# A rebuilt prologue in a fused cross-attention and ternary feed-forward kernel: rotary table spread by TensorE, first stacks written inside SBUF

## The chip, the cores and the metric

The kernel runs on one core of one Trainium2 chip. The metric is the device time of one execution in microseconds (us). The engines are TensorE (PE: matrix products and transposes), VectorE (DVE), ScalarE (ACT), GpSimd (POOL) and SyncE (SP), which here only issues transfers; ACT issues a few as well.

## The reference

`x` is 4 x 512 x 512, the context 4 x 512 x 256, all float32, with two positions in [0, 1) per token. The core of it:

```
x = x + xattn(layernorm(x), ctx, pos, pos, Wq, Wkv, Wout, bout)
x = x + ffn(layernorm(x), w_fc, w_proj)

xattn: q = rope(xn @ Wq), k, v = split(ctx @ Wkv), k = rope(k)     # 32 heads of 16
       softmax(q k^T / 4) v @ Wout + bout
rope:  ang = pos * freqs (2 positions x 4 frequencies per head)
       (x1, x2) -> (x1 cos - x2 sin, x1 sin + x2 cos)
ffn:   bitlinear(gelu(bitlinear(x, w_fc)), w_proj)   # layer norm, ternary weights
```

## The kernel before

**Stages.** Attention runs first, as one stream over 32 groups (4 batches x 8 groups of 4 heads), then the feed-forward part with all weights in SBUF. For attention the rotated queries and keys are each split in a high part (float32r) and a low part (the rest), and both are stacked on the partitions, 64 rows per head, so that one float32r product over 64 rows gives full accuracy. A group's two tiles `q_st` and `k_st` are its *stacks*. `heads` makes 8 heads' queries or keys: a product on PE, a copy to `rot` on ACT, a swap of row pairs with a stream shuffle into `oth` on DVE, two products with the tables in `trig` and a sum, then `high` and `low`. `store` writes them to the DRAM tensors `q_d` and `k_d`, four row sets of 128 rows each, and `load_stacks` reads two groups' worth back in the stacked order.

**A group.** `logits` (L423) makes one unit of scores (128 queries x 512 keys for two heads), `maxima` (L437) takes their row maxima on DVE. After eight units `place_maxima` transposes the maxima, ACT copies them to `mrows`, and `exponentials` computes the scores transposed (L462), subtracts the maxima by a product with the selector `sel` (L470), and takes Exp on ACT (L474). `weigh` (L484) multiplies by the values. PSUM has three double banks `ps_s`, one `ps_v` for the weighted values and one `ps_t` for all other products.

**Order.** The order on each engine is the order of the program text (a manual schedule over all five engines). `put_off(k, f)` delays an instruction to turn `k`, `run(k)` emits it. In the stream a burst holds three units, and a queue of *chores* (products of later heads, values, projections) is worked off between them by a credit per burst. Logits run up to 12 units ahead of exponentials. In the prologue a chore is finished at once, and `prologue[0]` chooses banks and engines.

**The prologue before.** SP and ACT load x, positions and first weights. `trig_tables` computes the sines of all four batches in one 128 x 256 tile (six DVE instructions, two on ACT), writes them to `trig_d` in DRAM; `load_trig(0)` reads batch 0's tables back, broadcast to all heads. DVE then takes the layer norm statistics (`norm1`), normalises (`normed`), PE transposes (`tokens`). The first two `heads` calls for keys and queries are rotated on DVE, stored to DRAM, and stacks 0 and 1 are loaded from there. The fill is a loop of 11 turns: ten logits units, beside them the four `values` products of batch 0, in the last turn the first `place_maxima`. Then output weights are loaded and the stream begins. Stacks 2 and 3 are loaded in the first group of the stream.

Of the kernel before, what the change touches and what calls it, by code (L numbers as in the profile page):

```python
# [15 lines left out]
P = 128  # L16
HD = 16
# [14 lines left out]
def xattn_ffn(  # L32
# [27 lines left out]
    VS = HD + 1  # L60
    FB = F // 512
    XH = 3
    RATE, RATE_END = 1.3, 1.1
# [26 lines left out]
    rden_d = [dram.tile([NH, S], F32, name=f"rden_d{b}") for b in range(B)]  # L90
    trig_d = dram.tile([2, 2, HD // 2, B * S], F32, name="trig_d")

# [31 lines left out]

    TW = B * S // HD * 2
    trig_sb = apool.tile([P, 4, TW], F32, name="trig_sb", tag="es", bufs=NES)
    pos_sb = trig_sb[:, 0, :]
    load_x(0, 0, 1)  # L130
    for n in range(2):
        nc.scalar.dma_start(
            pos_sb[n * P // 2 : (n + 1) * P // 2, :],
            pos.rearrange("a (c w) -> a c w", w=TW)
            .unsqueeze(0)
            .to_broadcast([4, 2, B * S // TW, TW]),
        )
    for t in range(1, NT):
        load_x(0, t, 1)
    ctx_tiles[0] = apool.tile([P, KC, S], F32, name="c_sb0", tag="c_sb", bufs=1)  # L140
    nc.scalar.dma_start(ctx_tiles[0], ctxT[0].rearrange("(k p) s -> p k s", p=P))
    load_columns(wkv_sb, wkv, 0, P)
    load_columns(wq_sb, wq, 0, P)


    ident = const.tile([P, P], F32, name="ident")
    make_identity(nc, ident)
    ones = const.tile([P, P], F32, name="ones")
    nc.gpsimd.memset(ones, 1.0)
    mhalf = const.tile([P, NT], F32, name="mhalf")  # L150
# [9 lines left out]
    nc.vector.tensor_tensor(row, row, ident, ALU.mult)  # L160
    nc.vector.tensor_reduce(col[:, 0:1], row, AX.X, ALU.add)


# [29 lines left out]
    def rstd(var, scale, eps, n, name):  # L193

        r = small.tile([P, n], F32, name=name, tag=f"rstd{n}")
        nc.gpsimd.tensor_scalar(r, var, scale, eps, ALU.mult, ALU.add)  # L196
        nc.gpsimd.tensor_tensor(r, r, mhalf[:, :n], ALU.pow)
        return r
# [3 lines left out]

    def trig_tables():

        ang, turns, sines = (trig_sb[:, n, :] for n in range(1, 4))
        e = nc.vector
        e.tensor_scalar(ang, pos_sb, col[:, 0:1], col[:, 1:2], ALU.mult, ALU.add)
        e.tensor_scalar(turns, ang, 0.5 / math.pi, ROUND, ALU.mult, ALU.add)
        e.tensor_scalar(turns, turns, ROUND, None, ALU.subtract)
        for part in (TWO_PI_HI, TWO_PI_LO):  # L210
            e.scalar_tensor_tensor(ang, turns, -part, ang, ALU.mult, ALU.add)
        e.tensor_scalar(ang, ang, SIN_MAX, -SIN_MAX, ALU.min, ALU.max)
        half = P // 2
        nc.scalar.activation(sines, ang, AF.Sin)
        nc.scalar.activation(turns[half:, :], ang[half:, :], AF.Sin, scale=-1.0)
        for n, j, src in ((0, 0, sines), (0, 1, sines), (1, 0, turns), (1, 1, sines)):
            nc.sync.dma_start(
                trig_d[n, j].rearrange("r (c w) -> (r c) w", w=TW),
                src[n * half : (n + 1) * half, :],
            )  # L220

    def load_trig(b):
        for n in range(2):
            nc.sync.dma_start(
                trig[:, b % 2, n, :],
                trig_d[n]
                .rearrange("j r t -> (j r) t")[:, b * S : (b + 1) * S]
                .unsqueeze(0)
                .to_broadcast([P // HD, HD, S]),
            )  # L230
# [14 lines left out]

    def bank(name):
        if prologue[0]:
            return ps_s.tile([P, 2, S], F32, name=name, tag="s")[:, 0, :]
        return ps_t.tile([P, S], F32, name=name, tag="t")
# [18 lines left out]
    def normed(b, t):  # L268
        tt = b * NT + t
        mv, r = norms[b]  # L270
        xh[b, t] = apool.tile([P, D], F32, name=f"xh{tt}", tag="xh", bufs=XH)
        nc.vector.tensor_scalar(
            xh[b, t], x_sb[:, tt, :], mv[:, t, 0:1], r[:, t : t + 1], ALU.subtract, ALU.mult
        )
# [18 lines left out]
    class Chore:  # L293


        def __init__(self, name, steps, step, post, cost=1.0, ready=0):
            self.name, self.steps, self.step, self.post = name, steps, step, post
            self.cost, self.ready, self.done = cost, ready, 0

        def go(self):  # L300
            if self.done == 0:
                self.p = bank(self.name)
            self.step(self.p, self.done)
            self.done += 1
            return self.done == self.steps
# [27 lines left out]
    def heads(b, n, what):  # L333
# [9 lines left out]
        def post(p, k):  # L343
            e = nc.vector if prologue[0] else nc.gpsimd
            rot = apool.tile([P, S], F32, name=f"rot_{name}", tag="rot")
            oth = apool.tile([P, S], F32, name=f"oth_{name}", tag="oth")
            high = apool.tile([P, S], F32R, name=f"sh_{name}", tag="sh")
            low = apool.tile([P, S], F32, name=f"sl_{name}", tag="sl")
            dst = (q_d if what == "q" else k_d)[b][n * 4 * P : (n + 1) * 4 * P, :]
            rows = dst.rearrange("(p k) s -> k p s", k=4)  # L350

            def swap():
                nc.vector.stream_shuffle(oth, rot, SWAP)
                e.tensor_tensor(oth, oth, trig[:, b % 2, 1, :], ALU.mult)
                e.tensor_tensor(rot, rot, trig[:, b % 2, 0, :], ALU.mult)
                e.tensor_tensor(rot, rot, oth, ALU.add)
                if not prologue[0]:
                    e.tensor_copy(high, rot)
                    e.tensor_tensor(low, rot, high.bitcast(F32), ALU.subtract)

            def split():
                nc.scalar.copy(high, rot)
                e.tensor_tensor(low, rot, high.bitcast(F32), ALU.subtract)
# [7 lines left out]
            high_f = high.bitcast(F32)  # L371
            hs, ls = ((0, 2), (1, 3)) if what == "q" else ((0, 1), (2, 3))
            put_off(k + 1, lambda: nc.scalar.copy(rot, p))
            put_off(k + 1, swap, 1)
            if prologue[0]:
                put_off(k + 1, split, 1)
            d = 1 if prologue[0] else 4
            put_off(k + d, lambda: store(high_f, hs), 1)
            put_off(k + d + (not prologue[0]), lambda: store(low, ls), 1)

        return Chore(f"{what}p{name}", steps, step, post)

    def values(b, t):
# [289 lines left out]

    k0 = -1000

    def chore(c):
        nonlocal k0
        while not c.go():
            pass
        c.post(c.p, k0)  # L680
        k0 += 1
        run(k0)
        run(k0, 1)

    trig_tables()
    for t in range(NT):
        norm1(0, t)
    load_trig(0)
    load_columns(wkv_sb, wkv, D, 2 * D)
    load_columns(wkv_sb, wkv, P, D)  # L690
    load_columns(wq_sb, wq, P, D)
    for t in range(XH):
        normed(0, t)
    prologue[0] = False
    first_keys = heads(0, 0, "k")
    while not first_keys.go():
        pass
    prologue[0] = True
    for t in range(NT):
        chore(tokens(0, t))  # L700
        if t + XH < NT:
            normed(0, t + XH)
    first_keys.post(first_keys.p, k0)
    chore(heads(0, 0, "q"))
    load_stacks(0)
    load_stacks(1)
    for what in "kq":
        chore(heads(0, 1, what))
    make_sel()
    load_x(1)  # L710
    nc.sync.dma_start(bout_sb, bout.to_broadcast([P, D]))
    prologue[0] = False
    lps = {}
    fill = [values(0, t) for t in range(NT)]
    for n in range(FIRST + 1):
# [6 lines left out]
        run(k0, 1)  # L722
        if fill:
            if fill[0].go():
                fill[0].post(fill[0].p, k0)
                fill.pop(0)
# [4 lines left out]
    assert not fill  # L731
    nc.sync.dma_start(wout_sb, wout.rearrange("(k p) n -> p k n", p=P))
    k0 += 1
# [29 lines left out]
    def projections(b):  # L763
        return [projected(b, t, when((b + 1) * NG + 2, 4)) for t in range(NT)]

    queue = [heads(0, n, w) for n in (2, 3) for w in "kq"]
    queue += sum(prepared(1, when(2)), [])
# [9 lines left out]
    loads_behind = {  # L777
        f"kpk{b}_3": lambda b=b: (load_ctx(b + 1), load_trig(b + 1)) for b in range(B - 1)
    }
    wanted = []  # L780
# [6 lines left out]
    for k, burst in enumerate(bursts):  # L787
        run(k)
        for kind, s in burst:
# [8 lines left out]

            if i == 0 and u in (2, 5):
                wanted.append(2 + u // 4)  # L800
            if u == 6 and 4 <= i + 3 < n_groups:
                wanted.append(i + 3)
            while wanted and {(wanted[0] // NG, wanted[0] % NG // 2, w) for w in "kq"} <= stored:
                load_stacks(wanted.pop(0))
            if i in (0, 4) and u == 0:
                load_x(2 + i // 4)
            if u % 2 == 0 and (b == 0 and g == 0 or b < 2 and g == 5):
# [347 lines left out]
```

## Time and profile before

| | us |
|---|---|
| median of 3 runs (lowest, highest) | 858.34 (857.26, 858.89) |
| profiled execution | 856.57 |
| its span, first to last instruction | 854.8 |
| PE busy in the span | 812.2 |
| DVE, ACT, POOL busy | 619.7, 456.7, 287.1 |
| first logits product starts | 34.37 |
| first exponentials' product starts | 50.66 |
| last exponentials' product starts | 574.9 |

The span is that of one profiled execution; its time is 1.8 us longer than its span and 1.8 us under the median of the runs. PE's busy time includes products at a reduced clock, since the table counts time and not work. Times in the text are from the span's start.

### The profile page before, as it was taken

How to read it: one execution, taken by the hardware profiler on the slowest of the kernel's cores; microseconds unless marked ns; L12 is line 12 of the kernel's file. 1: busy time of each engine (PE TensorE's matmuls, PEld its weight loads, DVE VectorE, ACT ScalarE, POOL GpSimd, SP SyncE). 2: the span in 40 equal slices, each digit the busy share in tenths (PEclk: the TensorE clock that was granted, in tenths of full speed). 3: DMA queues.
4: the chain of work that ended last, by engine and by line, in shares of the span. 5: the costliest groups of instructions: out<-in, count | busy, mean ns of one | idle time of the engine just before them, and what ended most of it. 6: DMA issues, size and time to landing. Idle time of an engine off the chain costs nothing.

```text
span 854.8 us, 13868 instructions
## 1 busy us (share of the span) xinstructions
PE 812.2 (95%) x5364; PEld 428.3 (50%) x5364; DVE 619.7 (72%) x852; ACT 456.7 (53%) x603; POOL 287.1 (34%) x287
## 2 busy tenths in 40 slices
PE   4699999999999899999999999998999999999996
PEld 1134433344333333433333334336668888888885
DVE  4789778788878988878678877825455864864755
ACT  2146766665665545666555665576234544554442
POOL 3017274653833564586515731301000100100000
PEclk9799999999999999999999999999999999999999
DMA  6875777567586576967645657432000100100101
GB/s 205 303 286 194 259 259 228 186 217 262 191 301 200 167 252 220 308 211 264 208 149 183 221 205 272 158 119 98 1 1 1 49 1 1 50 0 1 50 1 49
DMA packets 75561, 135.25 MB, mean 158 GB/s; under 512 B 10728, under 2 KB 12648, under 8 KB 74984
## 3 DMA queue, kind: packets, MB, share of 16 engines
q1 hardware_dynamic: 75088, 133.72, 45.8%
q8 instruction: 42, 0.69, 0.3%
q10 hardware_dynamic: 408, 0.66, 0.2%
q14 instruction: 23, 0.19, 0.1%
HBM read 79.30 MB, written 55.05 MB: 157 GB/s over the span
## 4 chain that ended last, share of the span: by engine, by line
PE 78%; DVE 12%; DMA 6%; issue 1%; ACT 1%; SPq 1%; POOL 1%; ACTq 0%; DVEq 0%; POOLq 0%
PE hp L928 14%; PE fp L966 14%; PE av L484 12%; PE sp L462 7%; PE lp L423 7%; DVE mx L437 7%; PE sp L470 5%; PE qpq L285 4%; PE op L285 4%; PE vp L285 3%; PE kpk L285 3%; PE op L1047 2%; PE mtp L449 1%; DVE ws L583 1%; DMA c_sb<-in_ctxT 1%
## 5 line engine op out<-in xcount | busy, mean ns | idle before, releaser
L437 DVE TENSOR_REDUCE mx<-lp 128x2 f32<-128x1024 f32 x256 | 305.3, 1216 | 86.0 <-PE lp L423 85.6
L474 ACT ACTIVATE es<-sp 128x1024 f32<-128x1024 f32 x256 | 254.5, 1025 | 146.6 <-PE sp L470 138.3
L484 PE MATMUL av<-es,va 128*32 128x512 f32 x1024 | 136.0, 604 | 0.0
L462 PE MATMUL sp<-q_st,k_st 64*128 64x512 f32 x512 | 115.1, 446 | 8.9 <-DVE mx L437 7.7
L423 PE MATMUL lp<-k_st,q_st 64*128 64x512 f32 x512 | 113.0, 437 | 9.4 <-DMA q_st<-q_d 7.4
L936 ACT ACTIVATE h<-hp,gam_fc 128x512 f32<-128x512 f32 x64 | 44.0, 688 | 129.1 <-PE hp L928 129.1
L966 PE MATMUL fp<-wproj,hh 128*128 128x512 f32 x256 | 103.5, 404 | 0.0
L928 PE MATMUL hp<-dTh,wfc 128*128 128x512 f32 x256 | 100.4, 392 | 1.2 <-ACT dTh L657 1.2
L470 PE MATMUL sp<-mrows,sel 64*128 64x512 f32 x512 | 101.2, 390 | 0.2 <-ACT mrows L453 0.2
L966 PE MATMUL fp<-wproj,hl 128*128 128x512 f32 x256 | 101.1, 395 | 0.0
L928 PE MATMUL hp<-dTl,wfc 128*128 128x512 f32 x256 | 100.4, 392 | 0.2 <-DVE dTl L658 0.2
L955 DVE TENSOR_TENSOR acc<-acc,h 128x512 f32<-128x512 f32 x56 | 38.7, 691 | 73.5 <-ACT h L936 73.5
L462 PEld LDWEIGHTS sp<-q_st,k_st 64*128 64x128 f32 x512 | 48.0, 184 | 83.1 <-DVE mx L437 42.6
L423 PEld LDWEIGHTS lp<-k_st,q_st 64*128 64x128 f32 x512 | 48.3, 185 | 80.8 <-ACT es L474 40.3
L523 POOL TENSOR_TENSOR aT<-aT,rb 128x512 f32<-128x512 f32 x16 | 21.1, 1320 | 133.3 <-DMA rb<-rden_d 112.1
L285 PE MATMUL qpq<-xT,wq_sb 128*32 128x512 f32 x512 | 62.3, 594 | 0.8 <-ACT xT L321 0.7
L928 PEld LDWEIGHTS hp<-dTh,wfc 128*128 128x128 f32 x256 | 48.2, 188 | 12.6 <-ACT dTh L657 2.1
L966 PEld LDWEIGHTS fp<-wproj,hl 128*128 128x128 f32 x256 | 48.3, 189 | 11.3 <-issue 0.7
L966 PEld LDWEIGHTS fp<-wproj,hh 128*128 128x128 f32 x256 | 48.2, 188 | 11.2 <-issue 0.7
L928 PEld LDWEIGHTS hp<-dTl,wfc 128*128 128x128 f32 x256 | 48.1, 188 | 11.0 <-DVE dTl L658 0.5
L470 PEld LDWEIGHTS sp<-mrows,sel 64*128 64x128 f32 x512 | 48.5, 185 | 5.9 <-ACT mrows L453 0.9
L196 POOL TENSOR_SCALAR r_a<-mv 128x1 f32<-128x1 f32 x16 | 4.7, 292 | 130.3 <-DVE mv L633 130.3
(129 smaller groups left out, 1036.0 us busy)
## 6 DMA issues: line engine op xcount, KB each, us to landing
k_st<-k_d SPq DMA_DIRECT2D x32, 512.0 KB
q_st<-q_d SPq DMA_DIRECT2D x32, 512.0 KB
k_d<-sh_k SPq DMA_DIRECT2D x32, 256.0 KB
k_d<-sl_k SPq DMA_DIRECT2D x32, 256.0 KB
q_d<-sh_q SPq DMA_DIRECT2D x32, 256.0 KB
q_d<-sl_q SPq DMA_DIRECT2D x32, 256.0 KB
av_d<-avs SPq DMA_DIRECT2D x32, 256.0 KB
wm<-in_wfcT SPq DMA_DIRECT2D x16, 256.0 KB
```

The source lines that it names most:

```text
L285: nc.tensor.matmul(p[j * HP : (j + 1) * HP, :], w[:, j * HP : (j + 1) * HP], x, start=start, stop=stop,)
L423: nc.tensor.matmul(lp[:, h, :], q_st[i][rows, r, t * P : (t + 1) * P], k_st[i][rows, r, :], start=True, stop=True,)
L437: nc.vector.tensor_reduce(mx[i][:, t, :, r], lp, AX.X, ALU.max, negate=True)
L462: nc.tensor.matmul(sp[:, h, :], k_st[i][rows, r, c * P : (c + 1) * P], q_st[i][rows, r, :], start=True, stop=False,)
L470: nc.tensor.matmul(sp[:, h, :], sel[rows, r, :], mrows[i][rows, :], start=False, stop=True)
L474: nc.scalar.activation(es, sp, AF.Exp, scale=1.0 / math.sqrt(HD))
L484: nc.tensor.matmul(av[j * HP : (j + 1) * HP, :], va[b % 2][:, c, v0 : v0 + HP], es[r][:, h, :], start=c == 0, stop=c == NT - 1,)
L523: nc.gpsimd.tensor_tensor(aT[b][:, n, :], aT[b][:, n, :], rb, ALU.mult)
L928: nc.tensor.matmul(hp, wfc_sb[k][:, f * P : (f + 1) * P], dT[b][half][:, k, :], start=half == 0 and k == 0, stop=half == 1 and k == KD - 1,)
L936: nc.scalar.activation(hid[b, f], hp, AF.Gelu, scale=gam_fc[:, 0:1])
L955: nc.vector.tensor_tensor(acc[b][0], old, x, ALU.add)
L966: nc.tensor.matmul(outs[b][t], parts[b, f][half][:, t * P : (t + 1) * P], wproj_sb[f], start=half == 0 and f == 0, stop=half == 1 and f == ...
```

## The change

- **Positions and tables.** The positions of each batch come in a load of their own (four on the ACT queue). `first_trig` computes batch 0's sines only (64 columns), on 128 partitions as 16 rows x 8 chunks. DVE spreads them to a 128 x 512 tile that is zero outside each row's own chunk (`wide`), and PE multiplies that with a 0/1/-1 selector `pick` so that each partition gets its table row; ACT copies the result to `trig`. The tables of batches 1 to 3 are computed later and written to DRAM behind the second stack's load.
- **Warm-up.** 24 products of `ones` by `ones` run on PE ahead of it.
- **Loads.** All of x for batch 0, then context and weights, then x of batch 1 are issued by SP at the start. Bias, output weights and x of batches 2 and 3 are loaded in groups 2, 3, 4 and 8.
- **Statistics.** The variance's epsilon is added on DVE in the prologue, the power stays on POOL. All four normalised tiles are made in a row.
- **First heads and stacks.** `first_heads` rotates the first keys and queries on DVE (keys' cast on ACT, keys' low part on POOL). `first_stacks` writes stack 0 from SBUF to SBUF in 16 transfers of 32 partitions: high parts on the SP queue, low parts on the ACT queue. `second_stacks` writes the other half to DRAM and loads stack 1 from there.
- **Second heads** go through the ordinary `heads`, whose rotation now always runs on POOL. Stacks 2 and 3 are loaded ahead of the stream.
- **Fill.** The first values product runs ahead of the fill; the fill holds the other three, every second one in the `ps_v` bank, and the third keys' product, which leaves the stream's queue. A one-column Exp is emitted before the fill.

```diff
+    for b in range(B):
+        load_pos(nc.scalar, b)
+    for t in range(NT):
         load_x(0, t, 1)
-    nc.scalar.dma_start(ctx_tiles[0], ctxT[0].rearrange("(k p) s -> p k s", p=P))
+    load_ctx(0)
     load_columns(wkv_sb, wkv, 0, P)
     load_columns(wq_sb, wq, 0, P)
+    load_columns(wkv_sb, wkv, P, D)
+    load_columns(wq_sb, wq, P, D)
+    load_columns(wkv_sb, wkv, D, 2 * D)
+    load_x(1)
...
+    def first_trig():
+        at, ang, turns, sines = (trig_sb[:, n, 0, :] for n in range(4))
+        angles(ang, at, turns)
+        nc.scalar.activation(sines, ang, AF.Sin)
+        wide = apool.tile([P, S], F32, name="wide", tag="sl")
+        nc.vector.tensor_tensor(
+            wide.rearrange("p (c w) -> p c w", c=NC),
+            sines.unsqueeze(1).to_broadcast([P, NC, W0]),
+            by_chunk.unsqueeze(2).to_broadcast([P, NC, W0]),
+            ALU.mult,
+        )
+        tp = ps_s.tile([P, 2, S], F32, name="trig_p", tag="s")
+        for n in range(2):
+            product(tp[:, n, :], pick[:, n, :], wide, True, True)
+        for n in range(2):
+            nc.scalar.copy(trig[:, 0, n, :], tp[:, n, :])
...
+    def first_heads(what, p):
+        keys = what == "k"
...
+        nc.scalar.copy(rot, p)
+        e.tensor_tensor(low, p, trig[:, 0, 0, :], ALU.mult)
+        e.stream_shuffle(oth, rot, SWAP)
+        e.tensor_tensor(oth, oth, trig[:, 0, 1, :], ALU.mult)
+        e.tensor_tensor(rot, low, oth, ALU.add)
+        if keys:
+            nc.scalar.copy(high, rot)
+        else:
+            e.tensor_copy(high, rot)
+        (nc.gpsimd if keys else e).tensor_tensor(low, rot, high.bitcast(F32), ALU.subtract)
+        return high.bitcast(F32), low
+
+    def first_stacks(what, high, low):
...
+        for r in range(2):
+            for queue, part, ks in ((nc.sync, high, 0), (nc.scalar, low, 1)):
+                for k in PARTS[what][ks]:
+                    queue.dma_start(
+                        st.bitcast(F32)[k:P:4, r, :], part[r * HP : (r + 1) * HP, :]
+                    )
+
+    def second_stacks():
+        for what in "kq":
...
+            for part, ks in zip(parts[what], PARTS[what]):
+                for k in ks:
+                    nc.sync.dma_start(rows[k], part[2 * HP : 4 * HP, :])
+        load_stacks(1)
...
+    p = bank("warm")
+    for n in range(WARM):
+        product(p[:, 0:P], ones, ones, True, True)
+    first_trig()
+    for t in range(NT):
+        norm1(0, t)
+    for t in range(NT):
+        normed(0, t)
+    store_tables = trig_tables()
+    make_sel()
+    for t in range(NT):
+        c = tokens(0, t)
...
+    for n in range(2):
+        for what in "kq":
+            c = heads(0, n, what)
+            while not c.go():
+                pass
+            if n == 0:
+                parts[what] = first_heads(what, c.p)
+                if what == "q":
+                    first_stacks("k", *parts["k"])
+                continue
...
+            if what == "k":
+                first_stacks("q", *parts["q"])
+            run(k0, 1)
+    second_stacks()
+    store_tables()
...
+    fill = [values(0, t) for t in range(1, NT)] + [heads(0, 2, "k")]
+    for c in fill[::2]:
+        c.spare = True
...
-    nc.sync.dma_start(wout_sb, wout.rearrange("(k p) n -> p k n", p=P))
+    for i in (2, 3):
+        load_stacks(i)
```

## The prediction, made before the changed kernel ran

> **What bounds the kernel now.** The page first: TensorE (PE) is busy 95% of the span, and in its row of 40 slices only the first two are thin. The stretch table of the trace says how thin (columns: stretch, its length, busy time of PE, weight loads, DVE, ACT, POOL, then granted clock, DMA share, GB/s):
>
> ```profile
> 0.00:34.30 34.30, 14.79 (x112) 4.92 (x112) 20.84 (x44) 8.68 (x15) 7.24 (x20) 0.94 0.71 232
> 34.30:50.70 16.40, 15.57 (x90) 3.92 (x90) 11.80 (x15) 2.35 (x4) 0.00 (x0) 0.81 1.04 365
> 50.70:60.00 9.30, 8.30 (x59) 2.81 (x58) 9.23 (x13) 6.43 (x7) 0.00 (x0) 1.00 0.88 323
> 60.00:100.00 40.00, 40.00 (x312) 17.46 (x309) 35.25 (x46) 25.88 (x32) 24.39 (x22) 1.00 0.62 205
> ```
>
> From 60 us on PE has no gap: what comes before it is added to the end one for one. Before 34.3 us PE idles 19.5 us, and from 34.3 to 50.7 it is "busy" at a granted clock of 0.81. The chain of waits says for what (start, length, what):
>
> ```profile
> 1.93 4.24 DMA trig_sb<-in_pos
> ...
> 11.09 2.09 DMA trig_d<-trig_sb
> 13.20 0.03 issue
> 13.23 5.77 DMA trig<-trig_d
> ...
> 27.23 3.49 DMA q_d<-sl_q
> 30.74 0.03 issue
> 30.77 3.46 DMA q_st<-q_d
> 34.23 0.14 issue
> 34.37 0.80 PE lp L423 x2
> ```
>
> The five transfers take 4.24+2.09+5.77+3.49+3.46 = 19.0 us of the first 34.4: positions in, tables out to DRAM and back, rotated heads out and back. The timeline shows the slow clock in identical value products:
>
> ```profile
> 37.68 1.93 PE L285 MATMUL vp<-wkv_sb,c_sb 128*32 128x512 f32 x8
> 40.38 1.06 PE L285 MATMUL vp<-wkv_sb,c_sb 128*32 128x512 f32 x8
> ```
>
> Twice as long until about 40.3 us, after PE had sat idle from 27.2 to 34.3.
>
> **What the skill says.** "TensorE: Matmul & The Clock Gate", What's actually happening: the array runs at half rate after about 3.4 us idle, at full rate after about 3.4 us of work. The trace agrees: 1.93 against 1.06 us, and back to speed 6 us after work resumed. "DMA: Bandwidth & Descriptors", Why a DMA increments its semaphore by 16 and not by 1: a transfer runs on k engines, the largest k up to 16 that divides the slowest dimension of both sides; the old position load (slowest dimension 4) would use 4, the new one (8) 8, a 32-partition stack piece 16. No row of this trace shows k. "SBUF — State Buffer", Who interferes with whom: a DVE instruction with two SBUF inputs, or in a two-port mode, excludes a GpSimd one. The trace agrees in kind: at 70.67 us an xh took 1.35 us beside POOL against 0.54 alone. Row maxima read PSUM and stay at 1.22.
>
> **The change, step by step.** Call A the time at which batch 0's positions are in SBUF. Before it was 6.2, for two 64 KB loads issued until 2.5. Now ACT issues four loads of 32 KB, batch 0 first; the first issue before ended at 1.90, and the shortest landing in the rows is about 2.1 (trig_d), so 4.0. DVE's new selector work (two reduces at 0.29, four small products at about 0.2, behind the old row work that ends at 2.4) ends near 3.9. Taken: A = 4.5, bounds 3.9 and 6.2.
>
> *DVE and PE up to the heads.*
> - Angles of 64 elements instead of 256: 2.5 us becomes 1.4. Sine (0.42 for 256) 0.3, the spread product (a 128x512 tensor_tensor row) 0.69: A+2.5.
> - PE's warm-up is 24 products of 8 instructions at N=128: a quarter of 0.86 warm, so 0.22, or 0.43 cold; from about 1.0 with 4 us cold it ends near 8.3 (bound 11.3). Spreading takes two products, 1.7, ACT two copies of 0.6: tables ready near 11, needed at A+11.9 = 16.4. Free; at the upper bound 14 still is.
> - Statistics: 3.3 (8.70 to 12.0 in the old rows), small DVE add 0.2, POOL power 1.02: A+7.1. Four normalisations 1.91: A+9.0. Transposes end A+9.7, last copy A+10.3.
> - DVE goes on with angles of batches 1 to 3 (2.1) and the selector (0.7): A+11.9. These lie beside k's product (1.72, to A+11.4).
> - PE goes on: q 3.64 (A+15.0), k1 1.8, q1 3.6, first values 1.8: A+22.2.
>
> *Heads to stacks.* k on DVE: product, shuffle, product, sum = 0.69+0.75+0.69+0.69, A+14.8. ACT casts (0.62), POOL subtracts (1.3): A+16.8. q: product and shuffle behind ACT's late copy of q (A+16.05), product, sum, cast 0.45, subtract 0.69: A+19.4. The queue with most behind it is ACT's: it issues four low pieces of k when POOL is done, copies k1, then four low pieces of q. An issue costs 0.35 to 0.9 in the rows (k_d pairs 0.82, ctx 0.47); at 0.5: A+18.9, copy A+19.5, last issue A+21.5. SP's four high pieces of q are issued by A+20.4. Landing: 2.1 as for the 64 KB trig_d stores (bounds 1.5 and 3.5, q_d). Stacks stand at A+23.6 = 28.1. Gone are trig out and back (7.9) and q_d, q_st (7.0). Against 34.2: **6.1 us earlier**. With all bounds 26 to 32.
>
> *Fill, from first logit to first exponential.* Now 16.3 (34.37 to 50.66). PE rests only from 26.7 to 28.2, so it is warm: before, two value steps cost 0.87 too much and three logit pairs 0.3, 2.6 in all. Values now alternate between two banks, so the wait for ACT's copy that every second turn had (turns of 1.78 against 1.42) falls away. As many steps as before, none in the first turn: 0.43 + 8 x 1.45 + 0.43 + transposes 0.55 = 13.0. **3.3 us**. DVE needs 8 x 1.22 = 9.8 and fits. If stacks land after about 30.1, the rest exceeds 3.4 us and the gate may take this back.
>
> *Into the stream.* First exponential at 41.2 against 50.66: 9.4. The Exp table load (1.28 at 51.37) moves ahead; DVE is the full engine from 50 to 58, so I count 0.3 (0 to 1.2). The third keys' product (1.72 and its gaps) leaves the queue for the fill: 1.5 (0 to 1.9, as DVE is 88% busy there). Total 9.4+0.3+1.5 = **11.2**.
>
> *Edits taken at nothing.* Four x loads and all weights on SP ahead, about 4.5 MB at some 320 GB/s: done by 17, before the stacks; the first weights are needed near 14. Bias and output weights move from 40 us to groups 2 and 3, used in group 5 and later; PE's full stream hides them. Second stack: SP stores eight pieces behind the first stacks (to 28.3), landing 31.3, reload 3.5: 34.8, needed by logit 8 at 38.8: with 4 us the tightest cover. Sines of the other batches and their stores lie behind it, used from 75 us. Second heads on POOL: k1 from 24.9, six us each (60.21 to 66.20 for a k before), to 36.9; stores 0.9 and landing 3.5, loads 3.5: stack 2 at 44.5. Logit 16 needs it; before, that ran at 60.9, 10.3 after the first exponential, so 51.5. Cover 7 us; behind it on SP wait only weight loads for column sums.
>
> **Sum.** The profiled execution had a span of 854.8, 856.57 with what lies around it; 845.4 after. The median of runs was 858.34, 1.8 above: 858.34 - 11.2 = 847.1, forecast **847**.
>
> **Rivals.**
> 1. *Small pieces are slow* (chance 0.25): 0.9 per issue on ACT, landing 3.5, A = 6.2. Stacks at 33 in the extreme, typically 31: 3 us earlier, fill partly cold, gain 4 to 7: 851 to 854. For it: the first position load was 4.24 beside the x loads. Against: 32 rows of 2 KB and an idle DMA by then.
> 2. *The gain is given back later* (0.08): group work waits for other chains, as at 246.9 to 254.8 (denominators out and back) and at 328 (7.30 for c_sb), which shift with the loads. PE is idle 4.0 in 250 to 300; double that and 7 are left: 851.
> 3. *POOL makes stack 2 late* (0.06), **slower**. k1, q1 and k2 now follow one another on POOL. If DVE's two-input work excludes POOL and the two rotations last over 30 us instead of 12, logit 16 waits 11 us and all is gone; at 33 us it is 861. For it: the exclusion above. Against: DVE does PSUM maxima then, and POOL's rows stay at 1.28 to 1.35 beside them.
> 4. *Nothing happens* (0.04): logits still wait for a transfer as late as before, if positions land at 6.2, all bounds meet and PE is cold again: 857.
>
> The forecast's own case has 0.57. About 1.7 us (0.2%) can be told from no change by this measurement. Faster: 0.57+0.25+0.08 = 0.90; same 0.04; slower 0.06. Range: own case 843 to 850; with most of rivals 1 and 2, 842 to 855.
>
> **What would show it.** Right: no trig<-trig_d before the first logit, first logit at 27 to 30 and exponential at 40 to 43, value products at 1.06 throughout, PE gapless from 50. Wrong: value products of 1.93 again; ACT queue issues near 0.9; a PE wait on q_st or k_st near logit 8 or 16; POOL rows above 2 us while q1 is rotated; or gaps in 100 to 350 us grown by what the start won.

## The result, and the profile after

The changed kernel takes **844.46 us** (median of four runs, 843.32 to 846.18) against 858.0 for the kernel before beside it: ratio 0.984, interval 0.982 to 0.986. Its profiled execution took 843.32, with a span of 841.5: 13.3 less than before. Where they went is read off four products in both traces; the stream is counted from the first exponentials' product to the last product of the exponentials with `sel`, the feed-forward part from the first to the last `hp` product (`hp` are its products with `w_fc`, `fp` those with `w_proj`).

| us | before | after | won | forecast |
|---|---|---|---|---|
| first logits product | 34.4 | 30.1 | 4.3 | 6.1 |
| fill, to the first exponentials' product | 16.3 | 14.2 | 2.1 | 3.3 |
| stream | 524.6 | 521.4 | 3.2 | 1.8 |
| feed-forward part | 259.2 | 255.7 | 3.5 | 0 |
| gap and tail | 20.3 | 20.1 | 0.2 | 0 |

The total was forecast well, the parts were not: start and fill gave 3 us less and two places behind them 5 us more. The table compares one execution of each kernel, and the start of the old one varies: in two more profiles with the same start (`before_warm` and `before_shift` below) its first logit stands at 36.5 and 36.2, 2 us later than here. The stretch table of the kernel after, cut at its own first logit and first exponential (columns as in the prediction):

```profile
0.00:30.10 30.10, 24.05 (x338) 12.91 (x338) 21.93 (x51) 7.42 (x13) 10.13 (x22) 1.00 0.62 193
30.10:44.30 14.20, 12.99 (x88) 3.58 (x88) 12.35 (x15) 5.07 (x10) 9.50 (x9) 1.00 0.87 249
44.30:60.00 15.70, 14.58 (x106) 5.82 (x104) 14.30 (x22) 8.73 (x11) 5.97 (x7) 1.00 0.89 296
60.00:100.00 40.00, 39.69 (x308) 16.55 (x310) 33.89 (x41) 26.50 (x32) 19.93 (x18) 1.00 0.74 251
```

The granted clock (the share of full speed that PE was given) is 1.00 in all of them, where the fill before had 0.81. The timeline of PE shows the same in the products (start, length, what; in brackets the idle time before and what ended it):

```profile
26.89 1.90 PE L342 MATMUL vp<-wkv_sb,c_sb 128*32 128x512 f32 x16
30.09 0.51 PE L519 MATMUL lp<-k_st,q_st 64*128 64x512 f32 x2 [1.29 <-DMA q_st<-sl_q]
31.39 0.50 PE L519 MATMUL lp<-k_st,q_st 64*128 64x512 f32 x2 [0.80 <-DMA q_st<-sl_q]
31.82 1.06 PE L342 MATMUL vp<-wkv_sb,c_sb 128*32 128x512 f32 x8
...
39.95 0.49 PE L519 MATMUL lp<-k_st,q_st 64*128 64x512 f32 x2
40.37 1.06 PE L342 MATMUL kpk<-c_sb,wkv_sb 128*32 128x512 f32 x8
41.51 0.49 PE L519 MATMUL lp<-k_st,q_st 64*128 64x512 f32 x2
...
43.76 0.66 PE L545 MATMUL mtp<-ident,mparts 128*128 128x128 f32 x4 [0.34 <-ACT rot_k L428]
44.34 0.50 PE L558 MATMUL sp<-q_st,k_st 64*128 64x512 f32 x2
```

Value products take 1.06 from the first on, and turns follow each other in 1.42. The first logit waits only for the pieces of the first two heads; the second waits another 0.80 for the other pieces. The timeline of POOL and DVE a few microseconds after the start shows where the first 2.4 us of the forecast were lost:

```profile
2.86 3.88 POOL L212 MEMSET va<- 128x2240 f32 x2
2.88 4.06 DVE L177 TENSOR_SCALAR first_sb<-first_sb 128x64 f32<-128x64 f32 x4
6.86 0.30 DVE L232 TENSOR_SCALAR trig_sb<-trig_sb,col 128x64 f32<-128x64 f32 x1
```

Four products of 64 columns (L177) take 4.06 us, as long as POOL fills the two value tiles with ones beside them. Batch 0's angles start at 6.86, not at 4.5. The timeline of the issuing queues (length is that of all issues of the row):

```profile
26.47 2.79 SPq L465 DMA_DIRECT2D q_st<-sh_q  x4
27.20 2.41 ACTq L465 DMA_DIRECT2D q_st<-sl_q  x4
...
37.15 0.37 SPq L505 DMA_DIRECT2D q_st<-q_d  x1
```

A piece of 32 partitions costs 0.60 on ACT and 0.70 on SP to issue here (the keys' pieces before them 0.68 and 0.62, so it isn't a difference between the queues). The reload of stack 1, behind all of SP's pieces and the eight stores of the other halves, goes out at 37.15.

### The profile page after: what moved, and what is told of

It is laid out like the page before. It is cut to its first block, busy times and chain, and to the rows that moved or that the text cites. A ratio compares the mean times of both kernels' runs of the same rounds, so it can differ in the third digit from the quotient of the medians.

```text
span 841.5 us, 14323 instructions
## 1 busy us (share of the span) xinstructions
PE 813.5 (97%) x5572; PEld 434.7 (52%) x5572; DVE 616.3 (73%) x858; ACT 456.6 (54%) x604; POOL 299.9 (36%) x297
## 5 line engine op out<-in xcount | busy, mean ns | idle before, releaser
L1047 ACT ACTIVATE h<-hp,gam_fc 128x512 f32<-128x512 f32 x64 | 44.1, 690 | 125.6 <-PE hp L1039 125.6
L519 PEld LDWEIGHTS lp<-k_st,q_st 64*128 64x128 f32 x512 | 48.0, 184 | 74.0 <-ACT es L570 40.1
```

The source lines that it names most:

```text
L519: nc.tensor.matmul(lp[:, h, :], q_st[i][rows, r, t * P : (t + 1) * P], k_st[i][rows, r, :], start=True, stop=True,)
L1047: nc.scalar.activation(hid[b, f], hp, AF.Gelu, scale=gam_fc[:, 0:1])
```

## The experiments

Times are medians, ratios are to the kernel before on the same chip, and "exponential" is the first exponentials' product.

### POOL's filling of the value tiles cut down

```diff
-        nc.gpsimd.memset(va_i, 1.0)
+        nc.gpsimd.memset(
+            va_i[:, :, 0 : NH * VS].rearrange("p t (h d) -> p t h d", d=VS)[:, :, :, HD:VS], 1.0
+        )
+        nc.gpsimd.memset(va_i[:, :, NH * VS : VW], 1.0)
```

> The changed kernel with one edit: POOL sets only the ones columns of the two value tiles (and their 16 spare columns) instead of the whole tiles. Theory (POOL held DVE): in the changed kernel the four selector products of L177 took 4.06 us for work of about 0.8, while POOL's 3.88 us fill of the value tiles ran; without it they end near 3.9, the angles start at 4.5 to 5 instead of 6.86, the first logit moves from 30.1 to about 28 and the time falls by about 2 us, to 842.5. Rival (positions are late anyway, since ACT's four issues last until 3.9): the selector products get short but the angles still start at 6.5 or later, first logit at 29.7 or later, time 844 to 845.

842.9 us (0.983, 0.981 to 0.984): 1.6 less than the changed kernel, but the two intervals touch, so the gain is read from the trace and not from the median. The timeline of DVE in this kernel:

```profile
2.89 0.85 DVE L177 TENSOR_SCALAR first_sb<-first_sb 128x64 f32<-128x64 f32 x4
4.68 0.32 DVE L235 TENSOR_SCALAR trig_sb<-trig_sb,col 128x64 f32<-128x64 f32 x1 [0.94 <-DMA trig_sb<-in_pos]
```

And PE's at logit 8:

```profile
40.66 0.50 PE L522 MATMUL lp<-k_st,q_st 64*128 64x512 f32 x2 [1.40 <-DVE mparts L541]
```

The same four products take 0.85: POOL had held DVE for 3.2 us. "SBUF — State Buffer", Who interferes with whom, in the Trainium skill says that a DVE tensor_scalar can enter a two-port mode, and that whichever of DVE and GpSimd takes the shared ports first blocks the other wholly; this pair of traces agrees. Now the positions end the wait, at 4.68: the A = 4.5 of the prediction was right for the transfer and wrong for DVE. The first logit comes at 27.9, 2.2 earlier, but the exponential only 0.8 (43.5). Logit 8, the first of stack 1, waits 1.40. The row names `mparts`, which was done at 39.96, 0.7 before. What it waited for must be stack 1, whose `q_st` reload SP issues at 35.75, 4.9 before; no row shows the landing itself. In the changed kernel SP issues the reload at 37.15 and logit 8 runs 4.4 later, at 41.51, with almost no cover left where the prediction saw 4 us.

### First stacks through DRAM; first tables through DRAM

Two parts of the change undone, one at a time. In the first, `first_stacks` writes the heads to `q_d` and `k_d` and reads stack 0 back:

```diff
-                    queue.dma_start(
-                        st.bitcast(F32)[k:P:4, r, :], part[r * HP : (r + 1) * HP, :]
-                    )
+                queue.dma_start(rows[k], part[0 : 2 * HP, :])
+        if what == "q":
+            load_stacks(0)
```

> The changed kernel with stack 0 written to DRAM and read back, on the same two queues, instead of inside SBUF. Theory (the bounce cost a round trip and let PE cool): first logit at 34.5 to 37 instead of 30.1, [...]first value products at 1.9 us again, first exponential 8 to 10 later than 44.3, time 852 to 855. Rival (the reload is mostly hidden, because fewer issues are needed): first logit at 32 to 33, PE warm, time 847.

852.59 us (0.993, 0.992 to 0.995). The timeline of PE:

```profile
14.56 2.59 PE L372 MATMUL xtp<-ident,xh 128*128 128x128 f32 x16 [3.19 <-DVE xh L329]
...
28.53 1.89 PE L342 MATMUL vp<-wkv_sb,c_sb 128*32 128x512 f32 x16
38.20 1.22 PE L518 MATMUL lp<-k_st,q_st 64*128 64x512 f32 x4 [7.78 <-DMA q_st<-q_d]
39.35 1.93 PE L342 MATMUL vp<-wkv_sb,c_sb 128*32 128x512 f32 x8
```

PE rests 7.8 us and works at half speed afterwards. The span is 851.0, 9.5 more: 8.1 up to the first logit and 1.1 in the fill. Not all of the 8.1 is the edit's. This execution ran slow products before the edit's place too (the same 16 transposes took 2.09 in the changed kernel), and the first values product stands 1.6 later (28.53 for 26.89). So writing inside SBUF is worth about 8 us of span.

In the second, batch 0's tables take the old way:

```diff
-        at, ang, turns, sines = (trig_sb[:, n, 0, :] for n in range(4))
+        at, ang, turns, sines = (trig_sb[:, n, :, :] for n in range(4))
...
+        load_trig(0)
+        return
```

> The changed kernel with the old table route: sines of all four batches at once, written to DRAM on the SP queue and batch 0 read back; the rest as in the change. Theory (the spread by PE is worth what the DRAM trip takes): the tables stand at 22 to 24 us because the trip takes 8 us and lies behind 4.5 MB of loads on the same queue; DVE's first rotation starts there instead of at 19.2, first logit 3 to 5 later, time 848 to 850. Rival (the tables were not what the rotation waited for): they stand by 19.5, first logit within 0.7 of 30.1, time 844 to 845.5.

852.95 us (0.994, 0.992 to 0.995). The timeline of PE:

```profile
35.04 0.80 PE L528 MATMUL lp<-k_st,q_st 64*128 64x512 f32 x2 [2.81 <-DMA q_st<-sl_q]
36.66 0.80 PE L528 MATMUL lp<-k_st,q_st 64*128 64x512 f32 x2 [0.82 <-DMA q_st<-sl_q]
37.38 1.93 PE L351 MATMUL vp<-wkv_sb,c_sb 128*32 128x512 f32 x8
39.25 0.79 PE L528 MATMUL lp<-k_st,q_st 64*128 64x512 f32 x2
39.97 1.93 PE L351 MATMUL vp<-wkv_sb,c_sb 128*32 128x512 f32 x8
```

First logit 4.9 later, fill 2.5 longer: 7.8 of span. The fill has the same products as in the changed kernel and no new wait; all of the 2.5 lies in its first turns, two value products at 1.93 for 1.06 and logit pairs at 0.80 for 0.50. That is what the clock costs in a fill.

Of the 13.3 us, 3.8 stay without the stacks' part and 5.5 without the tables', 3.5 of them in the feed-forward part. The two losses don't add up to the gain, and neither part undone is the old kernel's: the tables' trip now lies behind 4.5 MB of loads on the same queue (its reload is issued at 18.82), and both kernels have their first logit later than the 34.4 of the old one's profile.

### The clock of the fill: PE kept busy in the old kernel

```diff
+    p = ps_v.tile([P, S], F32, name="warm", tag="v")
+    for n in range(28):
+        product(p[:, 0:P], ones, ones, True, True)
```

> The kernel before with 28 small products of ones (about 6 us) put on PE between its last head product and its first logit, so that PE does not rest there. Theory (clock): granted clock 1.0 from 34.3, first value products at 1.06 us instead of 1.93, first exponential near 48.3 instead of 50.7, time 2.3 less than before, 855.7. Rival (the fill is paced by DVE and copies, the clock is a symptom): first exponential within 0.7 of 50.7, time as before. Its feed-forward part, which is the same code as before, also tells whether the 3.6 us that the changed kernel was shorter there belongs to the change: it should be near 259 us from first to last hidden product if so, anything from 255 to 259 if it varies by itself.

858.71 us over 12 runs (1.000, 0.998 to 1.001): no difference. In its profile the products ended at 34.13, stack 0 came only at 36.5, PE rested 2.36 and the first value products took 1.87 and 1.54. The warmth was gone again, so this run says nothing on the forecast's 2.6 us for the clock; the fill with the tables through DRAM, 2.5 longer at the slow clock, says it. Here a rest of 2.36 was followed by slow products.

### The feed-forward part: only the place of its tiles

Nothing in the change touches that part, and yet all its products are shorter. What it shares with the rest is SBUF: the result of the one-column Exp is a new tile in the small pool, and in the program's allocation `hh` begins at byte 174496 of each partition instead of 174368. The other tiles of the feed-forward pool move with it by the same 128 bytes; `wproj` and the operands of the `hp` products stay where they were. In the old kernel with such a tile and nothing else:

```diff
+    nc.gpsimd.memset(small.tile([P, 1], F32, name="exp_1", tag="exp_1"), 0.0)
```

> The kernel before with one small tile more in the pool of small tiles (one column, four buffers), set once by POOL in the prologue and never read. It moves the feed-forward pool's tiles (h, hh, hl, acc and so on) by 128 bytes per partition, to where they lie in the changed kernel, whose Exp preload has such a tile. Nothing else changes. Theory (place): the feed-forward part's 3.5 us, which all four kernels with the tile gained and both without it did not, come from where its tiles lie: first to last hidden product 255.7 instead of 259.2, time 3.5 less than before, 855. Rival (program): it comes from another trait of the changed program, so 259.2 stays and the time is that of before within 1.

And the changed kernel without it, the Exp's result going to a tile that exists anyway:

```diff
-        small.tile([P, 1], F32, name="exp_1", tag="exp_1"), ones[:, 0:1], AF.Exp
+        small.tile([P, 1], F32, name="exp_1", tag="gelu_1"), ones[:, 0:1], AF.Exp
```

> The changed kernel with the Exp preload's result written to the buffer of the later Gelu preload, so that the small pool and with it the feed-forward tiles lie where they lay before. Theory (place): first to last hidden product 259.2, time 3.5 above the changed kernel, 848. Rival (program): 255.7, time 844.5. First logit and first exponential stay at 30.1 and 44.3 in both.

The old kernel shifted: 854.22 (0.996, 0.994 to 0.997), feed-forward part 255.8. The changed kernel not shifted: 849.81 (0.990, 0.988 to 0.993), feed-forward part 260.9. The groups by line (count, busy us, mean ns, idle before) within the feed-forward part, first of the kernel before:

```profile
L966 PE MATMUL fp<-wproj,hh 128*128 128x512 f32 x232 | 93.9, 405 | 0.0
L966 PE MATMUL fp<-wproj,hl 128*128 128x512 f32 x232 | 91.7, 395 | 0.0
```

The kernel before, shifted:

```profile
L967 PE MATMUL fp<-wproj,hh 128*128 128x512 f32 x236 | 94.3, 400 | 0.0
L967 PE MATMUL fp<-wproj,hl 128*128 128x512 f32 x236 | 91.9, 390 | 0.0
```

The changed kernel:

```profile
L1077 PE MATMUL fp<-wproj,hh 128*128 128x512 f32 x223 | 89.2, 400 | 0.0
L1077 PE MATMUL fp<-wproj,hl 128*128 128x512 f32 x224 | 87.3, 390 | 0.0
```

The changed kernel, not shifted:

```profile
L1077 PE MATMUL fp<-wproj,hh 128*128 128x512 f32 x232 | 93.9, 405 | 0.0
L1077 PE MATMUL fp<-wproj,hl 128*128 128x512 f32 x233 | 92.1, 395 | 0.0
```

Five nanoseconds on each of 512 `fp` products are 2.6 us, and some two on each of 512 `hp` products 1 us: the 3.5. Shown both ways, the time follows the place of the pool's tiles, not the work. (Of the 260.9, some 1.7 is a stretch at a granted clock of 0.94.) Which tile does it, and why, is open: `hp` changes too, and none of its operands has moved.

### Second stack in fewer stores, and keys ahead of the transposes

Both hold the cut filling of the value tiles. The first also writes stack 1's halves to DRAM in four stores instead of eight:

```diff
-            for part, ks in zip(parts[what], PARTS[what]):
-                for k in ks:
-                    nc.sync.dma_start(rows[k], part[2 * HP : 4 * HP, :])
+            for part, (k, l) in zip(parts[what], PARTS[what]):
+                nc.sync.dma_start(
+                    rows[:, k : l + 1 : l - k, :],
+                    part[2 * HP : 4 * HP, :].unsqueeze(1).to_broadcast([2 * HP, 2, S]),
+                )
```

> The ones-columns kernel (va_ones) and the eight stores of the second stacks merged into four (one for both row sets of a part). Theory (stack 1 has become the late thing): in va_ones logit 8 waited about 1.4 us, since stack 1's q reload was issued at 35.75 and landed near 40.6; with four issues fewer on SP it is issued near 33.5, logit 8 comes at 39.2 and the first exponential near 42.1 instead of 43.5; time 1.4 less than va_ones, 841.5. Rival (the wait at logit 8 is of another thing, or a merged store takes as long to issue as two): first exponential still at 43.2 or later.

843.65 us (0.982, 0.979 to 0.985), exponential at 44.1. The reload of stack 1 is issued 0.9 earlier than in the first experiment (34.84 against 35.75) and logit 8 no longer waits, but the first stacks' last pieces land later, beside the merged stores. Nor does the reload gain the 2.2 us that my theory gave to four issues fewer: SP now waits 3.7 us for the last store to land before it (0.7 in the first experiment). The timeline of PE:

```profile
27.78 0.50 PE L524 MATMUL lp<-k_st,q_st 64*128 64x512 f32 x2 [1.75 <-ACT rot_q L431]
29.72 0.50 PE L524 MATMUL lp<-k_st,q_st 64*128 64x512 f32 x2 [1.44 <-DMA q_st<-sl_q]
30.15 1.87 PE L345 MATMUL vp<-wkv_sb,c_sb 128*32 128x512 f32 x8
```

The second logit waits 1.44 instead of 0.81 and the clock falls: one wait taken away, another put in its place. The rival is borne out.

The second also makes the keys' product before the transposes and rotates the keys before the angles of the other batches:

```diff
+    ck = heads(0, 0, "k")
+    ck.spare = True
+    while not ck.go():
+        pass
...
-    store_tables = trig_tables()
+    keys = first_heads("k", ck.p)
```

> The merged kernel and the first keys' product ahead of the transposes (in the spare bank), their rotation right behind the normalised tiles, the angles of batches 1 to 3 behind the queries' rotation. Theory (the first heads are a chain of PE and DVE in which the keys come too late): DVE rotates keys from 13.7 and queries from about 18.1 instead of 17 and 21; first logit at 25 to 25.7, now held by PE's own products, first exponential near 39, time 4 less than merged, 837.5. Rival (context and its weights land after 10.5, or the stacks' transfers then meet the loads of x): first logit at 27 or later, time 840 or more.

843.65 us (0.984, 0.980 to 0.987), first logit 27.8, exponential 42.0: the rival's case again, not the 837.5 of my theory. The keys' product waits 1.5 for `wkv` (until 11.05) and the transposes stand behind it, so the queries' product begins at 15.7, no earlier than without the edit (15.55), and the first logit, as before, waits 1.57 for the queries' last pieces. The edit helps only where the weights are there in time: in the last experiment below they came at 9.90, the queries' product began at 14.55 and the first logit stood at 26.2.

### No warm-up

```diff
-    p = bank("warm")
-    for n in range(WARM):
-        product(p[:, 0:P], ones, ones, True, True)
```

> The changed kernel without the 24 warm-up products of ones by ones; all else, and all that it computes, stays. My theory (as priced in the prediction, where the warm-up was counted as free): the two spread products and the 16 transposes run at the slow clock, at about 3.5 us instead of 1.9 and 3.7 instead of 2.1, and since the tables are not what the first keys wait for and the warmth is made up again by the keys' and queries' products, the first logit moves by 0 to 1 us (30.1 to 31.1); time 844.0 to 846. Rival: with positions landing late the products ahead of the queries are a chain, so the cold clock goes through: first logit +1.6 to 3.5, at 31.7 to 33.6, and 846.5 to 848.

846.34 us (0.987, 0.985 to 0.989). The timeline of PE:

```profile
9.45 3.58 PE L342 MATMUL trig_p<-wide,first_sb 128*32 128x512 f32 x16 [9.45 <-DVE wide L247]
14.56 2.09 PE L372 MATMUL xtp<-ident,xh 128*128 128x128 f32 x16 [1.53 <-DVE xh L329]
```

The spread products run cold, the transposes do not: the first logit stands at 30.1 as in the changed kernel, so the warm-up hides nothing here. The profiled span is 2.1 longer, all of it in the stream, where `sp` waits for row maxima 6.1 us between 240 and 370 against 3.8. Whether the median's 1.9 us comes from the missing products or from chance is open; the two intervals overlap.

### Second heads on DVE instead of POOL

```diff
-            e = nc.gpsimd
+            e = nc.vector if prologue[0] else nc.gpsimd
```

> The changed kernel with the second heads (k1, q1) rotated on DVE instead of POOL; nothing else is changed. My theory: POOL's rotation from 28.3 to 40.1 us is covered by logit 16, so taking it away gains nothing, and DVE, which has 8 maxima of 1.22 us in a fill of 14.2 us, gets some 7 to 8 us more of rotation (8 steps of 0.69 to 0.75 and two splits). What lies before the first maximum is hidden, what lies between is not: first exponential 2 to 6 us later (44.3 -> 46 to 50), time 846 to 850. Rival (the third rival of the prediction, POOL as the limit of the second stacks): stacks 2 and 3 come sooner and POOL's share of the time shows: first exponential as before and group work from 50 us on gains 1 us or more, time 842 to 844.

852.14 us (0.994, 0.992 to 0.996), more than my theory gave; the rival falls. The timeline of PE:

```profile
14.56 3.67 PE L372 MATMUL xtp<-ident,xh 128*128 128x128 f32 x16 [3.18 <-DVE xh L329]
18.16 2.96 PE L342 MATMUL kpk<-c_sb,wkv_sb 128*32 128x512 f32 x16
...
32.67 0.50 PE L519 MATMUL lp<-k_st,q_st 64*128 64x512 f32 x2 [1.25 <-DMA q_st<-sl_q]
```

And of DVE:

```profile
37.66 0.69 DVE L418 TENSOR_TENSOR sl_q<-rot_q,sh_q 128x512 f32<-128x512 f32 x1 [0.38 <-DMA k_d<-sl_k]
38.27 9.13 DVE L533 TENSOR_REDUCE mx<-lp 128x2 f32<-128x1024 f32 x8
```

Three things add up. DVE rotates until 38.27 and only then takes eight maxima in a row, and the first turns run at the slow clock as well, so the fill is 16.8 instead of 14.2; how much of that is DVE's, this run doesn't part. The stream is 2.2 longer, for which I have no cause. And the first logit is 2.6 later, from before the edit: transposes 3.67 instead of 2.09, keys' product 2.96 instead of 1.92. That is the clock, after the same rest of 3.18 that left it warm in the changed kernel:

```profile
14.55 2.09 PE L372 MATMUL xtp<-ident,xh 128*128 128x128 f32 x16 [3.18 <-DVE xh L329]
```

Only the profiled execution is known to have started cold, so the median's 7.7 can't be split in the same way.

### Third keys back in the stream

```diff
-    fill = [values(0, t) for t in range(1, NT)] + [heads(0, 2, "k")]
+    fill = [values(0, t) for t in range(1, NT)]
...
-    queue = [heads(0, n, w) for n, w in ((2, "q"), (3, "k"), (3, "q"))]
+    queue = [heads(0, n, w) for n, w in ((2, "k"), (2, "q"), (3, "k"), (3, "q"))]
```

> The changed kernel with the third keys' product put back into the stream's queue, so the fill holds the three values products only. The prediction booked 1.5 us (0 to 1.9) for taking it out of the stream. My theory: the stretch from first to last exponentials' product grows by 1.5 to 1.9 (521.4 -> 522.9 to 523.3), and the fill gives little of it back, since logit 8 waits for stack 1 at about 41 us whatever PE does before: first exponential 0 to 0.5 earlier. Time 845.5 to 846.5. Rival A (the fill is bound by PE's work): fill shorter by 1.8 (14.2 -> 12.4), stream longer by 1.8, time unchanged at 844.5. Rival B (the product had cover in the stream, and the 1.5 was never there): stream unchanged at 521.4, first exponential 0 to 1.8 earlier, time 842.7 to 844.5.

845.9 us (0.987, 0.984 to 0.990). The profiled execution has the cold start too. The timeline of PE:

```profile
14.56 3.04 PE L372 MATMUL xtp<-ident,xh 128*128 128x128 f32 x16 [3.18 <-DVE xh L329]
...
43.78 0.73 PE L519 MATMUL lp<-k_st,q_st 64*128 64x512 f32 x4 [1.83 <-DVE mparts L538]
```

The fill is 13.4, 0.8 shorter and not 1.8: logit 8 waits 1.83, until 4.8 us after the reload's issue at 39.01 (4.9 in the first experiment), as my theory had it. The stream is 525.8, 4.4 longer. Its PE busy time is 4.7 longer, 1.7 to 1.9 for the product and the rest at a lowered clock (0.82 in its first 9.3 us). The four runs split with the mean clock: 843.8 and 844.1 at 0.996, 847.7 and 848.4 at 0.993 and 0.991. So the median's +1.4 can't be put down to the product: two runs at the higher clock are no longer than the changed kernel. What moving it is worth stays open.

### The edits put together, and a third place for the tiles

The cut filling, the early keys with the eight single stores, and a pad at the head of the feed-forward pool:

```diff
+    nc.gpsimd.memset(fpool.tile([P, 24], F32, name="pad", bufs=1), 0.0)
```

> The changed kernel with three edits put together: GpSimd sets only the columns of ones in the value tiles; the first keys' product runs ahead of the transposes in a bank of its own and the keys are rotated before the angles of the other batches; and an unused tile of 96 bytes per partition at the head of the feed-forward pool moves the tiles behind it by another 96 bytes, so that the tile hh begins at a multiple of 256. Prologue, by the runs of these edits: first logit 27 to 27.8, first exponential 41.5 to 42.5 (44.3 in the changed kernel), and 2 us of gain. Feed-forward part, from first to last hidden product: 255.7 if the place of the old kernel (32 above a multiple of 256) is the exception, about 259 if the gain needs the place of the changed kernel (160 above a multiple of 256, as its other operands have). Time 842.0 in the first case, 845.5 in the second.

845.04 us (0.986, 0.984 to 0.987). First logit 26.2, exponential 41.8: 3.9 and 2.5 us ahead of the changed kernel. The fill loses 1.4 of the 3.9, at a clock that fell after two short rests. The timeline of PE:

```profile
26.24 0.49 PE L525 MATMUL lp<-k_st,q_st 64*128 64x512 f32 x2 [1.18 <-DMA q_st<-sl_q]
27.43 0.50 PE L525 MATMUL lp<-k_st,q_st 64*128 64x512 f32 x2 [0.69 <-DMA q_st<-sl_q]
27.86 1.78 PE L345 MATMUL vp<-wkv_sb,c_sb 128*32 128x512 f32 x8
```

The feed-forward part gives back more than that, 259.9 instead of 255.7. The groups by line:

```profile
L1091 PE MATMUL fp<-wproj,hh 128*128 128x512 f32 x217 | 88.1, 406 | 0.0
...
L1091 PE MATMUL fp<-wproj,hl 128*128 128x512 f32 x217 | 85.9, 396 | 0.0
```

So of three places of `hh`, two (0 and 32 above a multiple of 256) are slow, and only the changed kernel's (160 above) is fast. The early keys without the pad kept the fast place and had the shortest profiled span of all, 839.4; no kernel is faster than the changed one clear of the noise.

## Why the prediction was right, and where it was not

The forecast was 847, in a range of 842 to 855, with 0.90 for faster; 844.46 came out. Direction, range and the bounding chain hold. The sum came so near because its errors cancel, and that is luck: start and fill gave 3 us less than forecast, stream and feed-forward part 5 us more. With its tiles in the old place the changed kernel took 849.81, 8.2 less than before and not 11.2: inside the range still, but not near 847.

- **The marks:** value products at 1.06 and no tables through DRAM ahead of the first logit, as said; the first logit at 30.1 is at the late end of "27 to 30", and the exponential at 44.3 outside "40 to 43". PE isn't quite gapless from 50: it rests 0.24 us in 50 to 60 and 0.31 in 60 to 100. Of the marks of being wrong, ACT's issues stayed at 0.60 to 0.68 and the wait near logit 8 was 0.13.
- **What bounded the kernel: right.** Undone one at a time, stacks and tables through DRAM put the first logit at 38.2 (1.6 of it a slow start) and 35.0. One reading behind it was too wide: "From 60 us on PE has no gap" was read from 60 to 100 alone; in the old kernel PE rests 6.4 us between 250 and 350 and 4.5 between there and the stream's end.
- **A, positions in SBUF: right (4.68 for 4.5), but DVE was not free.** The mis-sized term is the selector work, ending at 3.9 in the forecast and at 6.86 in the trace: four products priced at 0.2 each took 4.06 beside POOL's fill. The prediction named this exclusion for two-input work against rotations and did not look for it here. Loss 2.4.
- **From A on: right.** With A = 6.86 the forecast's steps give keys rotated at 21.7, the keys' low part at 23.7, the queries' at 26.3, the last issue at 28.4, stacks at 30.5. The trace: 22.0, 24.0, 27.2, 29.6, and 30.1 for the logit, which needs only the first two heads' pieces; the others are there at 31.4. (The queries' steps as listed add up to A+20.0 and not A+19.4, so 26.9 for the 27.2 measured.)
- **Issue price of the small pieces: 0.5 was too low.** It measured 0.60 to 0.70. Rival 1 is borne out in kind, not in size.
- **Fill: 13.0 forecast, 14.2 measured.** The terms left out are 0.80 (second logit waits for its own pieces), 0.13 ahead of logit 8 and 0.34 (transposes wait for ACT's copy of `rot_k`): 1.27. DVE fits. The clock is 1.00 as said, and its size is borne out: with the tables through DRAM the same fill runs 2.5 longer at the slow clock, where 2.6 was booked. But "PE rests only from 26.7 to 28.2, so it is warm" was partly luck: rests of 1.18 and 0.69 were followed by slow products in the last experiment, rests of 1.29 and 0.80 in the changed kernel by a fast one.
- **Tightest cover: right place, wrong size.** Stack 1 was put at 34.8. Its reload is issued only at 37.15: SP's eight stores start at 29.3 instead of 24.9 and take 6.0 us instead of 3.4. And the reload lands some 4.4 to 4.9 after its issue instead of 3.5. The cover of 4 us was almost none, and most of an earlier start could not be cashed in.
- **Stream: 1.8 forecast, 3.2 measured.** PE's busy time fell by 1.65 (511.95 to 510.30), about the product moved out. The other 1.55 is idle time, all of it in the 100 us from 250 on (6.4 before, 4.6 after), where other kernels of this study show 3.2 to 6.9: it isn't shown to be the change's.
- **Feed-forward part: 0 forecast, 3.5 measured.** The step that failed is "edits taken at nothing": a new tile of one column moves the feed-forward pool's tiles, and by their place that part takes 255.7 or 259.2.
- **Rival 3, POOL as the limit: false.** POOL's rows stayed at 1.27 to 1.28 while k1 and q1 were rotated (28.3 to 40.1), and no PE wait on a stack appears at logit 16. Rivals 2 and 4 did not happen.
- **Warm-up free: right**, and it bought nothing that the trace shows.

## What to carry to other kernels

Price a small instruction by its neighbours too: a cheap DVE product beside a long GpSimd fill can cost five times its row. When a start is moved forward, work out the second transfer's cover with the queue's measured issue times and the measured time to landing, because that transfer becomes the bound. And before crediting an edit with a gain in code that it does not touch, compare mean times of the same matrix products and the places of their tiles.

## What the hardware showed that I had not expected

- **A product's rate follows the place of tiles in SBUF.** The same 128x512 product takes 400 or 405 ns with `hh` and 390 or 395 with `hl` when the feed-forward pool's tiles move by 128 bytes per partition; 96 bytes more make it 406 and 396. In sum 3.5 to 4.2 us in 850. Which of the tiles does it, and how, no run shows.
- **A rest of PE lies on an edge.** "TensorE: Matmul & The Clock Gate", What's actually happening, says that the activity window runs freely, so that the same kernel meets it at another phase each time. The traces agree: after 3.18 us of rest the 16 transposes took 2.09 in the changed kernel, and 2.59, 3.04 and 3.67 in three that are the same up to there. Shorter rests were followed by slow value products too: one of 2.36 by 1.87, 1.75 and 1.44 with a logit between them by 1.87, 1.18 and 0.69 by 1.78. That fixes no length below which a rest is safe. A cold start was worth 1.6 to 2.6 us at the first logit, as much as most edits of this study.
